# A graph layer with a running maximum over edges: later node search, casts on ScalarE, other end shares

## The chip, the cores and the metric

The kernel runs on one core of one Trainium2 chip. Its engines work side by side, each through its own list of instructions in order: TensorE (PE, and PEld for its weight loads), VectorE (DVE), ScalarE (ACT), GpSimd (POOL) and SyncE (SP), which only issues transfers. The metric is device time in microseconds of one execution.

## The reference

`N = 6250` nodes with rows of `D = 256` floats, `E = 100000` edges sorted by destination. For each edge a message is made, each node takes the largest of those that arrive, adds it to its row and normalises.

```python
x_src, x_dst = x[src], x[dst]
theta_x = (x_dst - x_src) @ theta_w.T + theta_b
phi_x = x_src @ phi_w.T + phi_b
e = relu(theta_x + phi_x)
out = segment_max(e, dst, num_segments=N)
out = where(isfinite(out), out, 0.0)
y = x + out
x = (y - mean(y)) / sqrt(var(y) + 1e-5)          # over the last axis
```

## The kernel before

The part of a message that hangs on the source is `B = x (phi - theta)^T`, one row per node. The part that hangs on the destination is the same for all edges of a node, so the kernel takes the maximum over `B[src]` first, and adds `x theta^T` and the biases, applies relu, adds `x` and normalises at the end. What has to be done fast is the maximum of 100000 rows by node. The kernel does it in three ways.

**First part.** The first 1130 nodes' edges are cut into 128 chunks of 146 steps, one chunk per partition. GpSimd gathers the rows of `B` by indirect transfers (L525, eight steps to a group), and VectorE runs a running maximum along each chunk (`run`, L687) that starts anew where the node changes. To read out a node's maximum one must know at which chunk and step its last edge stands: `node_place(j)` finds this for 128 nodes at a time, in nine blocks: two VectorE operations make a one-hot of the chunk (L843, L844), a matmul fetches that chunk's list of nodes (L846), and two `Sign` activations with an accumulated sum count how many entries lie before the node (L849); a copy takes the chunk's start (L852). `places_1` turns the counts into places. `chunk_heads` finds which chunks begin inside a node (L868 on), which `tails_1` (L889 on) needs to carry maxima across chunks.

**Second part, slots.** The other 5120 nodes are 128 partitions by 40 tiles. The rows of `B` are cut into 17 ranges of sources, the slots. `choice(s0)` picks, for two slots at a time (nine batches), at most one edge per node and slot: it marks the edges of a slot (L1016), takes minima (L1020 to L1025) to an int16 row number `at` (L1027), casts it to float in `chosen` (L1028), strikes that edge out (L1030, and L1034, which multiplies the marks of edges not yet used into `unused`). `wanted(s0)` transposes the codes by TensorE (L1041), copies them by ScalarE (L1043) and stores them. `slot_part`, in 85 chunks, loads the codes of one slot for eight tiles (L1080), lets ScalarE make one-hot matrices (an `Abs`, L1087, three times for 1024 columns each, then one `Relu`, L1090; later VectorE makes one of the three, L1085), multiplies them by the slot's rows of `B` on TensorE (24 matmuls, L1097) and takes the maximum into `acc` (ScalarE's copy L1106 for the first slot, then VectorE, L1108).

**Second part, list.** Edges that no slot took are counted and packed into a list of 233 steps (`list_pieces`, L1192 on: which are left, L1194; a cast to float, L1196; a scan that counts them, L1197; their ranks subtracted, L1206, and shifted by 20 bits, L1216; then a compaction by steps, L1225 and L1228). The list is gathered and reduced like the first part (30 groups, `run` with part 2, each group's maxima stored by SyncE at L699).

**Order.** Instructions of an engine run in the order in which the program issues them, apart from a few that `behind_in_order` puts behind a named one. The main program interleaves by hand: `next_group_1` issues a group of gathers of the first part, the running maxima of the group before, one `node_place` and some slot chunks. It is called from the loop over the list's pieces and after it. Then follow `places_1`, `tails_1` and the loop over the 30 list groups, in which the remaining slot chunks are spread evenly, with two shares of the first part's end from group 10 on. GpSimd's gathers wait for the rows that they overwrite.

**End.** `rows_of` and `normalise` handle a share of 8, 4 or 2 tiles: gathers of the maxima, matmuls with `theta` (L1335, L1338, L1347), VectorE adds (L1348, L1349, L1352, with the row's sum), the mean (L1365), ScalarE squares with their sum (L1368), then the variance (L1373), its inverse root with one Newton step (`inverse_root`, L423 to L429), the shift (L1375), and the result by ScalarE (L1383) or, for half the tiles of the last sixteen, VectorE (L1379), and the store (L1389). At the end the shares' widths are

```python
widths = [STEPS] * (TILES // STEPS - 2) + [4, 4, 4, 2, 2]
```

and two tiles are one piece of work; pieces and norms of different shares interleave.

## Time and profile before

| | us |
|---|---|
| three runs | 808.33, 814.1 (median), 823.09 |
| the profiled execution | 809.64 |
| its span, first to last instruction | 807.7 |

The mean granted TensorE clock of the profiled run is 0.913 of full speed. A row of a group of instructions has the line, the engine, the operation, output and inputs with their shapes, the count, then the busy time in us and the mean of one in ns, and behind the second bar the idle time of that engine just before these instructions with what ended most of it. A row of the timeline has start and length in us, and in brackets the idle time ahead with its releaser.

### The profile page before, as it was taken

What the parts mean: (1) busy time and instruction counts of PE and PEld (TensorE: products, weight loads), DVE (VectorE), ACT (ScalarE), POOL (GpSimd) and SP (SyncE); (2) the same over time, 40 slices, a digit from 0 to 9 for tenths busy, and PEclk for the clock granted to TensorE, in tenths of its full rate; (3) what the DMA queues carried; (4) which work ended last, traced back from release to release, by engine and by line L of the source; (5) the groups of instructions that cost most, each with busy time, mean ns of one, the idle gap of its engine ahead of it and who ended that gap; (6) DMA issues with size and microseconds to landing.
All of it is one profiled execution on the core that took longest, in us unless ns stands there. A gap on an engine that the chain in (4) does not pass through costs nothing.

```text
span 807.7 us, 9215 instructions
## 1 busy us (share of the span) xinstructions
PE 650.3 (81%) x2720; PEld 513.5 (64%) x2720; DVE 609.6 (75%) x1185; ACT 493.6 (61%) x576; POOL 475.1 (59%) x465
## 2 busy tenths in 40 slices
PE   5999787888874689399895988978999598677881
PEld 4888565656663478287774776756777376455771
DVE  7999989899956397278694686856698468783776
ACT  1446788997955375267574666745487377520666
POOL 7801888885676644436576766756656575425640
PEclk9999898999996989799997999989999899887896
DMA  8996638566685568346775777856858569644664
GB/s 275 310 367 223 187 107 265 161 186 221 217 266 187 160 225 288 104 131 210 232 243 166 229 266 264 291 169 214 250 175 268 169 204 318 210 151 124 206 239 159
DMA packets 60365, 174.40 MB, mean 216 GB/s; under 512 B 11995, under 2 KB 19956, under 8 KB 53268
## 3 DMA queue, kind: packets, MB, share of 16 engines
q1 hardware_dynamic: 37240, 109.25, 39.3%
q0 software_dynamic: 20944, 57.62, 24.2%
q10 hardware_dynamic: 2124, 6.88, 2.4%
q8 instruction: 23, 0.38, 0.2%
q14 instruction: 34, 0.28, 0.1%
HBM read 105.52 MB, written 68.18 MB: 215 GB/s over the span
## 4 chain that ended last, share of the span: by engine, by line
PE 42%; DVE 18%; issue 13%; another core or an unknown queue 11%; ACT 9%; DMA 4%; POOL 2%; DVEq 0%; SPq 0%; ACTq 0%; POOLq 0%
PE ps_f L1097 32%; PE ps_b L779 6%; DVE g L687 6%; ACT hot L1087 3%; DVE acc L1108 3%; ACT hot L1090 3%; DMA g<-maxima,place 2%; POOL g L525 2%; DVE hot L1085 1%; PE ps_e L1338 1%; ACT x_f L1383 1%; DVE x_f L1352 1%; DMA g<-b_rows,list_src 1%; DVE g L1348 1%
## 5 line engine op out<-in xcount | busy, mean ns | idle before, releaser
L1097 PE MATMUL ps_f<-hot,terms 128*128 128x512 f32 x1960 | 497.9, 412 | 92.7 <-ACT hot L1090 33.1
L1097 PEld LDWEIGHTS ps_f<-hot,terms 128*128 128x128 f32 x1960 | 383.7, 199 | 198.8 <-issue 47.1
L525 POOL DMA_INDIRECT g<-b_rows,list_src x232 | 234.0, 1009 | 154.1 <-DVE g L687 61.0
L1087 ACT ACTIVATE hot<-want,minus_row 128x1024 fp32r<-128x1024 f16 x187 | 205.3, 1145 | 186.7 <-remote 94.4
L1108 DVE TENSOR_TENSOR acc<-acc,ps_f 128x1024 f32<-128x1024 f32 x160 | 193.7, 1215 | 138.6 <-remote 75.9
L525 POOL DMA_INDIRECT g<-b_rows,src x130 | 153.8, 1183 | 97.0 <-DMA want<-chosen_rows 38.2
L687 DVE SCALAR_TENSOR_TENSOR g<-g,caps 128x256 f32<-128x256 f32 x376 | 180.3, 480 | 3.6
L1090 ACT ACTIVATE hot<-hot 128x2048 fp32r<-128x2048 f32 (+2 forms) x85 | 177.5, 2088 | 1.8
L779 PE MATMUL ps_b<-weights,x_t 128*128 128x256 f32 x260 | 62.8, 396 | 1.2 <-ACT x_t L767 0.6
L525 POOL DMA_INDIRECT g<-maxima,place x40 | 38.1, 953 | 42.9 <-DVE acc L1108 17.8
L779 PEld LDWEIGHTS ps_b<-weights,x_t 128*128 128x128 f32 x260 | 49.8, 197 | 10.4 <-ACT x_t L767 4.0
L1368 ACT ACTIVATE squares<-x_f,r 128x256 bf16<-128x256 f32 x49 | 24.2, 495 | 45.5 <-DVE r L1365 40.9
L1338 PE MATMUL ps_e<-weights,kept 128*128 128x256 f32 x160 | 42.9, 414 | 1.7 <-issue 1.7
L1085 DVE TENSOR_SCALAR hot<-want,row_id 128x1024 fp32r<-128x1024 f16 x58 | 44.1, 760 | 0.0
L1338 PEld LDWEIGHTS ps_e<-weights,kept 128*128 128x128 f32 x160 | 34.0, 212 | 7.2 <-issue 2.0
L1348 DVE TENSOR_TENSOR g<-g,ps_e 128x512 f32<-128x512 f32 x20 | 13.7, 685 | 25.9 <-remote 16.3
L782 ACT COPY b_sb<-ps_b 128x512 f32<-128x512 f32 (+1 forms) x25 | 14.5, 580 | 27.0 <-PE ps_b L779 19.0
L525 POOL DMA_INDIRECT g<-in_x_dram,src x16 | 25.3, 1582 | 5.6 <-issue 4.4
L1383 ACT ACTIVATE x_f<-x_f,r 128x256 f32<-128x256 f32 x41 | 21.5, 588 | 7.2 <-DVE r L1375 4.4
L767 ACT COPY x_t<-ps_xt 128x512 f32<-128x512 f32 (+1 forms) x33 | 18.4, 588 | 8.1 <-PE ps_xt L764 7.6
L1335 PE MATMUL ps_e<-bias_terms,pick 128*128 128x512 f32 x20 | 10.6, 528 | 9.9 <-DVE g L1348 8.6
L1228 DVE COPY_PREDICATED work<-words,work 128x288 int32<-128x288 int32 (+9 forms) x11 | 16.7, 1515 | 0.0
(253 smaller groups left out, 421.9 us busy)
## 6 DMA issues: line engine op xcount, KB each, us to landing
maxima<-g SPq DMA_DIRECT2D x47, 1024.0 KB
want<-chosen_rows SPq DMA_DIRECT2D x85, 256.0 KB
x_q<-in_x_dram SPq DMA_DIRECT2D x12, 512.0 KB
b_rows<-b_sb ACTq DMA_DIRECT2D x12, 512.0 KB
x_columns<-x_t SPq DMA_DIRECT2D x20, 256.0 KB
kept<-x_columns SPq DMA_DIRECT2D x10, 512.0 KB
raw<-b_rows SPq DMA_DIRECT2D x16, 256.0 KB
x_f<-in_x_dram SPq DMA_DIRECT2D x4, 1024.0 KB
```

Of the source, the lines that this page charges most:

```text
L525: one = nc.gpsimd.indirect_dma_start(out=to, out_offset=None, in_=table, in_offset=bass.IndirectOffsetOnAxis(ap=offsets, axis=0))
L687: one = nc.vector.scalar_tensor_tensor(g[:, k, :], last[part], caps[:, t : t + 1], g[:, k, :], op0=ALU.min, op1=ALU.max)
L779: nc.tensor.matmul(ps[:, h, :], x_t[:, h, k, :], weights[:, k, 0, :], start=(k == 0), stop=(k == KC - 1))
L1085: nc.vector.tensor_scalar(hot[:, b, :], want, row_id[:, b : b + 1], None, op0=ALU.is_equal)
L1087: nc.scalar.activation(hot[:, b, :], want, AF.Abs, bias=minus_row[:, b : b + 1], scale=1.0)
L1090: nc.scalar.activation(apart, apart.bitcast(FP), AF.Relu, bias=1.0, scale=-1.0)
L1097: nc.tensor.matmul(ps[:, w : w + 512], terms[:, part, b, h * P : (h + 1) * P], hot[:, b, w : w + 512], start=(i == 0), stop=(i == n - 1),)
L1108: one = nc.vector.tensor_tensor(to, to, ps, op=ALU.max)
L1338: nc.tensor.matmul(a[:, i, :], x_t[:, 2 * i + c, :], weights[:, c, 1, :], start=False, stop=(i == w - 1 and c == KC - 1))
L1348: nc.vector.tensor_tensor(some, some, ps[:, :w, :], op=ALU.max)
L1368: nc.scalar.activation(squares, x_f[:, k, :], AF.Square, bias=mean[:, k : k + 1], scale=1.0, accum_out=var[:, k : k + 1])
L1383: nc.scalar.activation(x_f[:, k, :], x_f[:, k, :], AF.Identity, bias=mean[:, k : k + 1], scale=inv[:, k : k + 1])
```

## The change

The parts of the diff, in the order of a run:

- `choice`: the cast of `at` to `chosen` goes from VectorE to ScalarE, and `at` gets three buffers. For the first slot pair `unused` is made by one product of the two slots' marks, where before it was filled with ones and multiplied twice.
- `list_pieces`: the cast of the left-over marks goes to ScalarE; ScalarE multiplies the ranks by 2^20 in advance, behind its last copy of B; VectorE then subtracts the count times 2^20 in one operation, and the shift goes.
- `ends_1` (formerly straight code), `node_place` and `places_1` move from the first part's groups into the loop over the list groups: `ends_1` to group 0, one `node_place` to each of groups 0 to 8, `places_1` to group 9. `chunk_heads` moves to directly ahead of `tails_1`.
- `run`: the list's last full group is stored in three pieces, after four, six and eight steps.
- `normalise`: the division by D goes into the squares' scale (1/16 ahead of squaring), eps into the root's bias, so the steps for the variance and for adding eps go.
- The end's widths become 4, 4, 8, 8, 8, 4, 2, 2 instead of 8, 8, 8, 4, 4, 4, 2, 2.

```diff
+ROOT_D = 16.0
@@ -605,7 +606,9 @@
     iota(minus_row, -P, 0, -1)
     iota(columns[:, 0, :], Q1, 0, 0)
     iota(columns[:, 1, :], 1, P * Q1, 0)
-    bad = const.tile([P, 10], FP, name="bad")
+    checks = const.tile([P, 11], FP, name="bad")
+    bad, eps = checks[:, :10], checks[:, 10:]
+    nc.vector.memset(eps, EPS)
     descents = search.tile([P, T + 1], FP, name="descents")
     below = search.tile([P, T + 1], FP, name="below")
@@ -677,7 +680,7 @@
     def run(part, g, n, caps, t0, to, gathers=(), carry_row=None):
-
+        stored, ends_at = 0, (4, 6) if t0 + n == LIST_CHUNK else ()
         for k in range(n):
             t = t0 + k if part == 1 else LIST_CHUNK - 1 - t0 - k
             if last[part] is not None:
@@ -695,8 +698,13 @@
                     behind_in_order(one, latest_part[0], "VectorE's order")
                 used.append(one.ins.name)
             last[part] = g[:, k, :]
+            if part == 2 and k + 1 in ends_at:
+                a, ends_at = ends_at[0], ends_at[1:]
+                nc.sync.dma_start(to[:, stored:a, :], g[:, stored:a, :])
+                stored = a
         latest_run[0] = one.ins.name
-        nc.sync.dma_start(to, g[:, :n, :])
+        if stored < n:
+            nc.sync.dma_start(to[:, stored:n, :], g[:, stored:n, :])
     def run_1(i, gathers=()):
         t0, n = groups[i]
@@ -779,7 +789,7 @@
                     nc.tensor.matmul(
                         ps[:, h, :], x_t[:, h, k, :], weights[:, k, 0, :], start=(k == 0), stop=(k == KC - 1)
                     )
-            nc.scalar.copy(to, ps[:, :n, :])
+            b_copied[0] = nc.scalar.copy(to, ps[:, :n, :]).ins.name
         def x_group(i):
             for q in range(0, STEPS, 2):
@@ -817,19 +827,22 @@
     iota(offset[:, :Q1], 1, 0, 0)
     nc.vector.memset(offset[:, Q1:], 0.0)
     first = const.tile([P, 1], FP, name="first")
-    nc.vector.tensor_copy(first, chunk[:, 0:1])
-    nc.vector.memset(first[0:1, :], -1.0)
-
     low = const.tile([P, NT1], FP, name="low")
-    nc.vector.tensor_scalar(low, offset, -1.0, first, op0=ALU.mult, op1=ALU.add)
     high = const.tile([P, NT1], FP, name="high")
-    nc.vector.tensor_scalar(high, offset, -1.0, after, op0=ALU.mult, op1=ALU.add)
-    nc.vector.tensor_scalar(
-        bad[:, 2:3], after, float(N1), ident[:, P - 1 :], op0=ALU.is_lt, op1=ALU.mult
-    )
     upper = const.tile([P, 2, NT1], FP, name="upper")
-    nc.vector.tensor_scalar(upper[:, 0, :], node_1, 0.5, None, op0=ALU.add)
-    nc.vector.tensor_scalar(upper[:, 1, :], node_1, -0.5, None, op0=ALU.add)
+
+    def ends_1():
+
+        nc.vector.tensor_copy(first, chunk[:, 0:1])
+        nc.vector.memset(first[0:1, :], -1.0)
+        nc.vector.tensor_scalar(low, offset, -1.0, first, op0=ALU.mult, op1=ALU.add)
+        nc.vector.tensor_scalar(high, offset, -1.0, after, op0=ALU.mult, op1=ALU.add)
+        nc.vector.tensor_scalar(
+            bad[:, 2:3], after, float(N1), ident[:, P - 1 :], op0=ALU.is_lt, op1=ALU.mult
+        )
+        nc.vector.tensor_scalar(upper[:, 0, :], node_1, 0.5, None, op0=ALU.add)
+        nc.vector.tensor_scalar(upper[:, 1, :], node_1, -0.5, None, op0=ALU.add)
+
     signs = const.tile([P, 2, NT1], FP, name="signs")
     origin = const.tile([P, NT1], FP, name="origin")
     place_1 = const.tile([P, NT1], I32, name="place_1")
@@ -938,8 +951,7 @@
         return part if len(shape) == 2 else part.rearrange("p (s n) -> p s n", s=shape[1])
     chosen = index.tile([P, NS, TILES], FP, name="chosen")
-    at = index.tile([P, BATCH_S, 1, TILES], I16, name="at")
-    nc.vector.memset(unused, 1)
+    nc.vector.memset(unused[:, CHOICE_R * TILES :], 1)
     def floor_of(to, value, divisor):
         nc.vector.tensor_scalar(
@@ -1017,6 +1029,7 @@
         lowest = wide_i16(BATCH_S * CHOICE_R * W, [P, BATCH_S, CHOICE_R * W // 2])
         low = lowest[:, :n, :]
+        at = index.tile([P, BATCH_S, 1, TILES], I16, name="at", bufs=3)
         least = lambda to, a, b: nc.vector.tensor_tensor(to, a, b, op=ALU.min)
         least(low, in_slot[:, :n, : 12 * W], in_slot[:, :n, 12 * W :])
         least(low[:, :, : 6 * W], low[:, :, : 6 * W], low[:, :, 6 * W :])
@@ -1025,13 +1038,15 @@
         least(low[:, :, :W], low[:, :, :W], low[:, :, 2 * W : 3 * W])
         nc.vector.tensor_scalar(at[:, :n, 0, :], low[:, :, :W], rows_in(s0), None, op0=ALU.min)
-        nc.vector.tensor_copy(chosen[:, s0 : s0 + n, :], at[:, :n, 0, :])
+        nc.scalar.copy(chosen[:, s0 : s0 + n, :], at[:, :n, 0, :])
         kept = in_slot.rearrange("p s (r j) -> p s r j", r=CHOICE_R)
         nc.vector.tensor_tensor(
             kept[:, :n], kept[:, :n], at[:, :n].to_broadcast([P, n, CHOICE_R, W]), op=ALU.not_equal
         )
         for i in range(n):
-            one = nc.vector.tensor_tensor(unused[:, all_ranks], unused[:, all_ranks], in_slot[:, i, :], op=ALU.mult)
+            rest = in_slot[:, 1, :] if s0 + i == 0 else unused[:, all_ranks]
+            if s0 + i != 1:
+                one = nc.vector.tensor_tensor(unused[:, all_ranks], rest, in_slot[:, i, :], op=ALU.mult)
         ahead_of_run[0] = one.ins.name
     def wanted(s0):
@@ -1193,7 +1208,9 @@
         left_over = wide_i16(3 * BATCH_S * CHOICE_R * TILES // 2, [P, TR])
         nc.vector.scalar_tensor_tensor(left_over, padded, float(SLOT * NS), unused, op0=ALU.is_lt, op1=ALU.mult)
         valid, count = work_1, work_2
-        nc.vector.tensor_copy(valid.rearrange(by_node, r=R), left_over.rearrange("p (r j) -> p j r", r=R))
+        nc.scalar.copy(valid.rearrange(by_node, r=R), left_over.rearrange("p (r j) -> p j r", r=R))
+        one = nc.scalar.activation(order, order, AF.Copy, scale=float(1 << 20))
+        behind_in_order(one, b_copied[0], "B ahead of the ranks")
         nc.vector.tensor_tensor_scan(count, valid, valid, 0.0, ALU.add, ALU.max)
         nc.vector.tensor_copy(n_list, count[:, TR - 1 :])
         sums = sums_of_lists()
@@ -1203,7 +1220,7 @@
         list_chunks(sums)
         nc.vector.tensor_scalar(bad[:, 3:4], n_list, float(OWN_LIST), None, op0=ALU.is_gt)
         distance, mask = order.bitcast(I32), count.bitcast(I32)
-        nc.vector.tensor_tensor(distance, order, count, op=ALU.subtract)
+        nc.vector.scalar_tensor_tensor(distance, count, -float(1 << 20), order, op0=ALU.mult, op1=ALU.add)
         nc.vector.tensor_scalar(mask, valid, -1.0, None, op0=ALU.mult)
         word = words.bitcast(I32)
         nc.vector.tensor_tensor(
@@ -1213,7 +1230,6 @@
             op=ALU.add,
         )
         done = valid.bitcast(I32)
-        nc.vector.tensor_scalar(distance, distance, 20, None, op0=ALU.logical_shift_left)
         nc.vector.tensor_tensor(done, word, distance, op=ALU.bitwise_or)
         nc.vector.tensor_tensor(done, done, mask, op=ALU.bitwise_and)
         yield
@@ -1362,17 +1380,21 @@
         shared = part == 2 and j0 >= TILES - 2 * STEPS
         r = work.tile([P, 5, STEPS], FP, name="r", bufs=4)
         mean, var, root, inv, step = (r[:, k, :n] for k in range(5))
-        nc.vector.tensor_scalar(mean, totals[:, :n], -1.0 / D, None, op0=ALU.mult)
+        nc.vector.tensor_scalar(mean, totals[:, :n], -1.0 / (D * ROOT_D), None, op0=ALU.mult)
         for k in range(n):
             squares = work.tile([P, D], BF, name="squares")
             nc.scalar.activation(
-                squares, x_f[:, k, :], AF.Square, bias=mean[:, k : k + 1], scale=1.0, accum_out=var[:, k : k + 1]
+                squares, x_f[:, k, :], AF.Square, bias=mean[:, k : k + 1], scale=1.0 / ROOT_D, accum_out=var[:, k : k + 1]
             )
             if k % 2 and k + 1 < n:
                 yield
-        nc.vector.tensor_scalar(var, var, 1.0 / D, None, op0=ALU.mult)
-        inverse_root(nc, inv, var, root, step)
-        nc.vector.tensor_tensor(mean, mean, inv, op=ALU.mult)
+        nc.scalar.activation(root, var, AF.Sqrt, bias=eps)
+        nc.vector.reciprocal(inv, root)
+        nc.vector.tensor_tensor(step, inv, inv, op=ALU.mult)
+        nc.vector.scalar_tensor_tensor(step, var, EPS, step, op0=ALU.add, op1=ALU.mult)
+        nc.vector.tensor_scalar(step, step, -0.5, 1.5, op0=ALU.mult, op1=ALU.add)
+        nc.vector.tensor_tensor(inv, inv, step, op=ALU.mult)
+        nc.vector.scalar_tensor_tensor(mean, mean, ROOT_D, inv, op0=ALU.mult, op1=ALU.mult)
         yield
         for k in range(n):
             if shared and k % 2:
@@ -1433,8 +1455,6 @@
             gathers = gather_group(i, b_rows)
             if i > X_GROUPS:
                 run_1(i - 1, gathers)
-        if todo:
-            node_place(todo.pop(0))
         fetch_parts(n)
     fill_table()
@@ -1448,7 +1468,6 @@
         run_1(i)
     for _ in range(2):
         next_group_1(0)
-    chunk_heads()
     for i, _ in enumerate(list_pieces()):
         if i == 14:
             dve_hots[0] = DVE_HOTS
@@ -1466,10 +1485,10 @@
     tables.close()
     x_ring = body.enter_context(tc.tile_pool(name="x_ring", bufs=X_RING, side="right"))
     kept_ring = body.enter_context(tc.tile_pool(name="kept_ring", bufs=3, side="right"))
-    while groups_1 or todo:
+    while groups_1:
         next_group_1(2)
     run_1(len(groups) - 1)
-    places_1()
+    chunk_heads()
     carried = tails_1()
     n_groups = LIST_GROUPS
     blocks_left = lambda: sum(blocks_in(s) for s, _ in parts)
@@ -1491,6 +1510,11 @@
             next(heads, None)
         if i == CARRY_AT:
             carry_row = gather_carry()
+            places_1()
+        if i == 0:
+            ends_1()
+        if todo:
+            node_place(todo.pop(0))
         g, gathers = gather_2(i * STEPS)
         if i:
             run(2, g_before, STEPS, caps_2, (i - 1) * STEPS, maxima_2t[i - 1], gathers)
@@ -1515,7 +1539,7 @@
     fetch.close()
     ps_end = body.enter_context(tc.tile_pool(name="ps_end", bufs=6, space=PSUM))
-    widths = [STEPS] * (TILES // STEPS - 2) + [4, 4, 4, 2, 2]
+    widths = [4, 4] + [STEPS] * (TILES // STEPS - 2) + [4, 2, 2]
     assert sum(widths) == TILES
     last_shares = [(2, sum(widths[:i]), n) for i, n in enumerate(widths)]
     at_end = Shares(lambda: ps_end.tile([P, 2 * D], FP, name="ps_e"))
```

More of the change, by code (lines that the diff above doesn't have):

```diff
@@ L768, in x_transposed @@
             return x_t
+        b_copied = [None]
         def b_of(to, rows, kept=None):
@@ L1295, in gather_carry @@
         return carry_row
+    assert ROOT_D * ROOT_D == D
     x_tiles = {}
```

## The prediction

> **What bounds the kernel now.** I read the page first (busy times, chain), then the waits, then a table of busy time by stage, then the groups and the timeline of the stages that the diff touches.
>
> ```profile
> span 807.7 us, 9215 instructions
> PE 650.3 (81%) x2720; PEld 513.5 (64%) x2720; DVE 609.6 (75%) x1185; ACT 493.6 (61%) x576; POOL 475.1 (59%) x465
> ...
> PE 42%; DVE 18%; issue 13%; another core or an unknown queue 11%; ACT 9%; DMA 4%; POOL 2%; DVEq 0%; SPq 0%; ACTq 0%; POOLq 0%
> ```
>
> No engine is full over the whole span. TensorE carries 42% of the chain that ended last, VectorE 18%, ScalarE 9%. These are means over unlike stages, so I cut the span at the first slot sums (98), the end of the list's making (240), the start of the list gathers (340) and the last slot maximum (722). Columns are start and end, length, busy time of the five engines with counts, granted clock, DMA share and GB/s.
>
> ```profile
> core 0: us, PE busy (x) PEld busy (x) DVE busy (x) ACT busy (x) POOL busy (x), PEclk, DMA share, GB/s
> 0.00:98.00 98.00, 83.11 (x408) 68.91 (x408) 90.43 (x183) 47.17 (x81) 48.70 (x56) 0.97 0.81 276
> 98.00:240.00 142.00, 120.55 (x483) 93.65 (x483) 127.95 (x254) 123.03 (x132) 104.79 (x85) 0.93 0.65 204
> 240.00:340.00 100.00, 64.53 (x254) 51.11 (x254) 60.31 (x105) 50.76 (x39) 56.34 (x60) 0.84 0.60 195
> 340.00:722.00 382.00, 325.85 (x1315) 253.83 (x1315) 278.36 (x445) 235.20 (x206) 229.07 (x227) 0.93 0.67 219
> 722.00:808.00 86.00, 56.25 (x260) 46.02 (x260) 52.57 (x201) 37.47 (x120) 36.21 (x38) 0.81 0.53 177
> ```
>
> VectorE sets the first stage (90.4 of 98). In the second VectorE (128), ScalarE (123) and TensorE (121 of 142) are all near full, and each is waited for by turns. In the list stage TensorE is busy 326 of 382 and the other two have room: 104 us on VectorE, 147 on ScalarE. The waits show by turns who is late:
>
> ```profile
> POOL g L525 <- DVE g L687: 82.4, 25, 18.7
> ACT hot L1087 <- remote: 94.4, 16, 14.3
> DVE acc L1108 <- remote: 75.9, 14, 10.7
> PE ps_f L1097 <- ACT hot L1090: 33.1, 16, 14.5
> PE ps L1041 <- DVE chosen L1028: 4.8, 1, 4.8
> ```
>
> Columns: total, times, longest. The two "remote" rows (170 us together) are ScalarE and VectorE waiting for something that the profile cannot name; each follows slot matmuls, so I read them as late releases by TensorE. No edit touches those matmuls: I leave this time where it is. The last row is one wait of the first stage that the change aims at.
>
> **The change, part by part.** The sum is made against the profiled run, 809.64 us (span 807.7). The three plain runs are 808.33, 814.1 and 823.09, so that run lies 4.5 below their median.
>
> *First stage: codes converted by ScalarE, one product less.*
>
> ```profile
> L1028 DVE CAST chosen<-at 128x80 f32<-128x80 int16 x8 | 1.6, 201 | 0.3
> L1034 DVE TENSOR_TENSOR unused<-unused,wide 128x960 int16<-128x960 int16 x17 | 11.2, 659 | 0.4
> L844 DVE SCALAR_TENSOR_TENSOR hot<-columns,high,hot 128x128 f32<-128x128 f32 x9 | 3.0, 337 | 0.0
> L843 DVE TENSOR_SCALAR hot<-columns,low 128x128 f32<-128x128 f32 x9 | 2.7, 299 | 0.9 <-PE ps L846 0.9
> ```
>
> ```profile
> 98.42 0.79 PE L1097 MATMUL ps_f<-hot,terms 128*128 128x512 f32 x1 [0.68 <-ACT g L782]
> ```
>
> This is the first slot sum, the end of the stage. By the pace of the batches six of the nine casts (L1028) lie before 98: 6 x 0.201 = 1.2 us off VectorE. The first two products (L1034) become one: 0.66 us. Of the node search, nine pairs of L843 and L844 (2.7 + 3.0 = 5.7 us), some two pairs run here (an estimate from the code's order): 1.3 us. Together 3.2 us off the engine that is 92% full. On ScalarE (47 of 98) the casts are a small matter, but they add a wait: a code now goes VectorE, ScalarE, TensorE, and the cast stands in ScalarE's order among the copies of B, so each copy behind it waits until VectorE has that batch. ScalarE has 51 us of idle time here, which covers this; uncovered, it would cost up to the one wait of 4.8 above, on the other side. I take -3, bounds 0 (transfers or GpSimd set this stage: the DMA share is 0.81) to -3.2, and +4.8 as the bad end.
>
> *Second stage: node search out, list's casts to ScalarE, shift gone.* The next rows are the groups of this stage, then its timeline on VectorE and GpSimd (start, length, operation, idle time before).
>
> ```profile
> L849 ACT ACTIVATE junk<-ps,upper 128x146 bf16<-128x146 f32 x18 | 6.7, 378 | 1.4 <-PE ps L846 1.0 <-issue 0.4
> L849 ACT ACTIVATION_READ_ACCUMULATOR junk<-ps,upper 128x1 f32 x18 | 3.6, 200 | 0.0
> L1106 ACT COPY acc<-ps_f 128x1024 f32<-128x1024 f32 x10 | 10.1, 1011 | 5.3 <-issue 3.6 <-PE ps_f L1097 1.6
> L846 PE MATMUL ps<-ids,hot 128*128 128x148 f32 x18 | 4.4, 326 | 1.2 <-DVE hot L844 1.2
> ...
> L1216 DVE TENSOR_SCALAR order<-order 128x1440 int32<-128x1440 int32 x1 | 0.9, 910 | 0.0
> ```
>
> ```profile
> 113.77 1.64 DVE L1194 SCALAR_TENSOR_TENSOR wide<-padded,unused 128x1440 int16<-128x1440 int16 x1
> ...
> 115.74 1.61 DVE L1196 CAST work<-wide 128x1440 f32<-128x1440 int16 x1
> ...
> 117.67 3.14 DVE L1197 TENSOR_TENSOR_SCAN work<-work 128x1440 f32<-128x1440 f32 x1
> ```
>
> ```profile
> 112.76 0.94 POOL L525 DMA_INDIRECT g<-b_rows,src  x1 [0.30 <-issue]
> 114.01 3.46 POOL L525 DMA_INDIRECT g<-b_rows,src  x1 [0.30 <-issue]
> 117.78 3.79 POOL L525 DMA_INDIRECT g<-b_rows,src  x1 [0.30 <-issue]
> ...
> 206.72 0.94 POOL L525 DMA_INDIRECT g<-b_rows,src  x1 [12.03 <-DVE g L687]
> ```
>
> VectorE loses the other seven pairs (5.7 x 7/9 = 4.4), the cast L1196 (1.6), the shift L1216 (0.9) and three small casts (0.6): 7.5 us. ScalarE loses the eighteen Signs, between 6.7 (accumulator reads beneath) and 10.3 us; I take 8, nearer the first because the recorded ends overlap. It gains the cast and the scaling of 1440 columns. No such row exists; by the 1024-column copy (1.011 us) each is 1.011 x 1440/1024 = 1.4 us, two 2.8. The three small casts lie between the accumulator read (0.20) and the 146-column Sign (0.38): 0.9 in all. So ScalarE goes from 123.0 to 123.0 - 8 + 2.8 + 0.9 = 118.7, 4.3 less. TensorE's 120.6 loses the eighteen search matmuls, 4.4 us. The stage can shrink by what the less relieved of the two loses, 4.3; I take -4, bounds 0 and -7.5. The new wait: the scan L1197 now waits for ScalarE's cast, which stands in its order behind one chunk's Relu; what is queued behind the scan on VectorE is the list's counting and the first part's running maxima, and GpSimd's gathers wait for those. At worst that is one such wait of a few us, inside the 0 end of this term. What becomes late next is TensorE: it has 21 us of idle time in this stage, so the gain has room.
>
> *Third stage.* It is a chain (last rows of the first part, tails, caps) with no engine above 65 of 100 us. The moved chunk heads add some 1 us of small VectorE work ahead of the tails, under 60 us of work in 100. It passes earlier gains on: 0.
>
> *List stage: the search comes in here.* Each of groups 0 to 8 gets two VectorE operations (0.64 us), a matmul pair on TensorE and two Signs on ScalarE (0.9 us). That is 8 us on ScalarE, which has 147 us idle, 6 us on VectorE, which has 104, and the 4.4 us on TensorE, which is the bound. I take +2, since TensorE's 56 us of idle time hide part. Queues passed: the search issues no DMA; SP's queue gets two more DMAs for the split store; GpSimd's first gather by these places comes after group 9, with a group's length (382/30 = 12.7 us) between. Lower bound 0, upper bound in the second rival.
>
> *Three-piece store.*
>
> ```profile
> 719.77 0.94 POOL L525 DMA_INDIRECT g<-maxima,place  x1 [17.79 <-DVE acc L1108]
> ```
>
> The first gather behind the list's store waits for VectorE's last slot maximum, not for the store, so an earlier store buys nothing while the slots end at 722: 0, bounds 0 and -1.5.
>
> *End: norm and shares.*
>
> ```profile
> 747.39 0.51 ACT L1368 ACTIVATE squares<-x_f,r 128x256 bf16<-128x256 f32 x1 [34.45 <-DVE r L1365]
> ...
> 788.94 5.03 ACT L1383 ACTIVATE x_f<-x_f,r 128x256 f32<-128x256 f32 x10 [1.38 <-DVE r L1375]
> ```
>
> ```profile
> L423 DVE TENSOR_SCALAR r<-r 128x8 f32<-128x8 f32 (+2 forms) x8 | 1.5, 189 | 0.0
> ...
> L1373 DVE TENSOR_SCALAR r<-r 128x8 f32<-128x8 f32 (+2 forms) x8 | 1.3, 161 | 0.0
> ```
>
> Two of nine VectorE steps of a norm go (L423, L1373): 2.8 us over eight norms, of which the last norm's 0.35 us is surely on the path, the rest only as far as VectorE is pressed (53 of 86). The widths matter more. ScalarE stands idle for 34 us until the first norm of eight tiles, then has a backlog: at 788.94 it applies ten tiles in 5 us, late in the stage. A first share of four tiles brings the first norm forward by two of twenty pieces; at (789 - 722)/20 = 3.4 us a piece that is 7 us of earlier work for ScalarE, and about half of the backlog (2.5 us) should be gone. 0.35 + 2.5 is 2.9: I take -3, bounds +2 (eight-wide shares now stand later, so the 4, 2, 2 at the end meet more unfinished work) and -6.
>
> Sum: -3 - 4 + 0 + 2 + 0 - 3 = -8, 809.6 - 8 = 801.6; I say 802.
>
> **The rivals.** *GpSimd sets the first 240 us.*
>
> ```profile
> L525 POOL DMA_INDIRECT g<-b_rows,src x130 | 153.8, 1183 | 97.0 <-DMA want<-chosen_rows 38.2
> ```
>
> The first part's 130 gathers take 1.18 us each, and two of them 3.46 and 3.79 where the neighbour takes 0.94. If their issue is the pace, less work on VectorE and ScalarE is only more waiting: the first two terms fall away, 809.6 + 2 - 3 = 808.6. Against it: at 206.72 GpSimd itself waits 12 us for a running maximum on VectorE. In this case the long gathers count: the one at 114.01 ends at 117.47, 0.12 us after the cast L1196 (117.35), the next at 121.57, 0.76 us after the scan (120.81). With the cast on ScalarE the first would end with L1194 at 115.41, 2 us sooner: 806.6. The Trainium skill ("SBUF — State Buffer", section "SBUF: two separate sides") calls this a lock: while VectorE holds the port pair that it shares with GpSimd, GpSimd writes no descriptors for its DMAs. The trace agrees for the cast by these 0.12 us; the scan's gather runs on for longer than the rule says. I give this rival 0.17.
>
> *The search stops ScalarE in the list stage (slower).* In the list stage a Sign stands in ScalarE's order between the slots' one-hots, and its matmul stands in TensorE's order behind a chunk's matmuls. If ScalarE has run ahead it must wait there for TensorE, and the next chunk's one-hots come late. A wait of TensorE on one-hots costs 33.1/16 = 2.1 us on the mean; nine of them 19 us in place of the +2, so 809.6 - 10 + 19 = 818.6. It decides against the change from 10/9 = 1.1 us a node on. For it: TensorE already waits sixteen times for L1090. Against: ScalarE is 62% busy here, and two buffers of one-hots keep it from running far ahead, so it mostly waits for the same releases already. 0.15.
>
> *More than the sum.* If the 12 us wait at 206.72 goes because VectorE's backlog of running maxima goes, stage two shrinks by the full 7.5, and if the end gives its 6: 809.6 - 3 - 7.5 + 2 - 6 = 795. 0.15.
>
> *The change doesn't do what it says*, since a scheduler places the moved work where it likes: the order of the built kernel has the nine searches among chunks 29 to 44, inside the list stage, so I give it nothing.
>
> **How the numbers follow.** The forecast has the remaining 0.53. The likeliest case gives 802. The range 788 to 820 holds it with its bounds, the GpSimd rival, the larger gain and most of the slower rival; below lies an end that gives more than 6 with a first stage that gives more than its casts, above a search of over 2.2 us a node. Two per cent of 814.1, about what these runs can tell from no change, puts the borders at 798 and 830. Faster: 0.12 of the larger gain and 0.15 out of the forecast's lower part, 0.27. Slower: 0.03 of the slower rival's tail and 0.06 for runs that spread as 823 did, 0.09. Same: 0.64.
>
> **What would show it.** First stage: the wait of L1041 shrinks from 4.8 and the slot sums begin some 3 us sooner than 98. Second: no Sign rows before 240, VectorE near 120 busy, the 12 us wait at 206.72 below 8, the list gathers 7 us sooner than now. List stage: from first list gather to last slot maximum 382 to 385 us; Signs with idle time in front of over 1 us each would prove the slower rival. End: 83 us, the first squares within 30 us of the last slot maximum, the ten-tile application gone. The prediction is wrong if the list stage grows by more than 6 us, or if the list gathers begin when they do now.

## The result, and the profile after

The changed kernel takes 819.92 us in the median of 20 executions (812.04 to 827.84), the kernel before 813.68 (799.94 to 828.91). The ratio is 1.0152 of the time before, 95% interval 1.0112 to 1.0193. Forecast were 802 us and a gain. The ratios, here and below, leave out executions over 1.5% above the fastest of their kernel (here 14 of the 20 of the kernel before and 2 of the changed one), while the medians are of all executions, by which the ratio would be 1.0077. The profiled execution of the changed kernel, 826.43 us (span 824.6), lies 6.5 above its median and that of the kernel before 4.0 below, so the two profiles differ by more than the kernels do.

The page, and the waits, of the changed kernel (total, times, longest):

```profile
span 824.6 us, 9185 instructions
PE 652.7 (79%) x2720; PEld 516.1 (63%) x2720; DVE 602.5 (73%) x1154; ACT 501.6 (61%) x587; POOL 489.9 (59%) x465
...
L526 POOL DMA_INDIRECT g<-b_rows,src x130 | 168.2, 1294 | 90.6 <-DMA want<-chosen_rows 41.0
```

```profile
ACT hot L1102 <- remote: 124.7, 17, 15.9
DVE acc L1123 <- remote: 123.9, 24, 15.8
```

VectorE has 7 us less to do, ScalarE 8 more. What was not foreseen is GpSimd: the same 130 gathers take 168.2 us where they took 153.8. The table by stretch shows where; the first fence is the kernel before, the second the changed one. The columns are those of the stage table above, and each stretch holds the list's compaction (eleven steps of a `TENSOR_SCALAR` and a `COPY_PREDICATED` on VectorE, L1225 and L1228 before, L1241 and L1244 after).

```profile
142.00:207.00 65.00, 55.67 (x223) 42.83 (x222) 60.94 (x87) 59.83 (x65) 42.92 (x35) 0.95 0.58 178
```

```profile
142.00:194.00 52.00, 48.07 (x202) 37.42 (x201) 52.00 (x70) 50.28 (x37) 45.65 (x21) 0.99 0.55 175
```

VectorE gets through the compaction in 52 us instead of 65, with no gap (52.00 of 52). In that time GpSimd issues 21 gathers of 2.2 us, where before it issued 35 of 1.2 us. The timeline of the changed kernel shows one such meeting after the other:

```profile
163.07 0.87 DVE L1241 TENSOR_SCALAR words<-work 128x1408 int32<-128x1408 int32 x1
165.79 1.75 DVE L1244 COPY_PREDICATED work<-words,work 128x1408 int32<-128x1408 int32 x1
171.76 0.86 DVE L1241 TENSOR_SCALAR words<-work 128x1376 int32<-128x1376 int32 x1
```

```profile
162.74 2.04 POOL L526 DMA_INDIRECT g<-b_rows,src  x1 [0.30 <-issue]
165.08 0.95 POOL L526 DMA_INDIRECT g<-b_rows,src  x1 [0.30 <-issue]
166.33 2.01 POOL L526 DMA_INDIRECT g<-b_rows,src  x1 [0.30 <-issue]
...
171.44 2.01 POOL L526 DMA_INDIRECT g<-b_rows,src  x1 [0.30 <-issue]
```

The three long gathers end at 164.78, 168.34 and 173.45, which is 0.84, 0.80 and 0.83 us after the ends of the three VectorE operations (163.94, 167.54, 172.62); the one that meets neither takes 0.95. No idle time of GpSimd over 1 us is left between 96 and 237: it sets the pace of the first part now. So the list is made 13 us earlier, and the first part, for whose rows its gathers wait, is later:

```profile
318.52 1.42 POOL L526 DMA_INDIRECT g<-b_rows,list_src  x1 [15.80 <-DVE g L690]
...
737.20 0.95 POOL L526 DMA_INDIRECT g<-maxima,place  x1 [18.93 <-DVE acc L1123]
```

The first list gather starts at 318.5 (before at 310.4), the first gather of the end at 737.2 (before at 719.8, the row in the prediction). Of the 16.9 us between the two spans 8.1 are there at the list's first gather, 9.3 come in the list stage, and the end gives 0.5 back. How much of this is the change and how much the draw, only more profiles can tell.

### The profile page after: what moved, and what is told of

It reads as the page before. It is cut to its first block, busy times and chain, and to the rows that moved or that the text cites. A ratio compares the mean times of both kernels' runs of the same rounds, so it can differ in the third digit from the quotient of the medians.

```text
span 824.6 us, 9185 instructions
## 1 busy us (share of the span) xinstructions
PE 652.7 (79%) x2720; PEld 516.1 (63%) x2720; DVE 602.5 (73%) x1154; ACT 501.6 (61%) x587; POOL 489.9 (59%) x465
## 4 chain that ended last, share of the span: by engine, by line
PE 38%; DVE 18%; issue 13%; another core or an unknown queue 12%; ACT 7%; DMA 6%; POOL 6%; DVEq 0%; POOLq 0%; ACTq 0%; SPq 0%
PE ps_f L1112 32%; POOL g L526 6%; DVE g L690 4%; DMA g<-b_rows,src 3%; PE ps_e L1356 2%; DVE acc L1123 2%; DVE words L999 2%; ACT hot L1102 2%; ACT hot L1105 1%; ACT squares L1386 1%; DMA g<-b_rows,list_src 1%; ACT x_f L1405 1%; DVE work L996 1%; DVE wide L1033 1%
## 5 line engine op out<-in xcount | busy, mean ns | idle before, releaser
L1112 PE MATMUL ps_f<-hot,terms 128*128 128x512 f32 x1960 | 506.9, 417 | 112.7 <-DVE acc L1123 32.1
L1112 PEld LDWEIGHTS ps_f<-hot,terms 128*128 128x128 f32 x1960 | 389.2, 202 | 221.6 <-issue 59.7
L1123 DVE TENSOR_TENSOR acc<-acc,ps_f 128x1024 f32<-128x1024 f32 x160 | 193.8, 1216 | 169.6 <-remote 123.9
L526 POOL DMA_INDIRECT g<-b_rows,src x130 | 168.2, 1294 | 90.6 <-DMA want<-chosen_rows 41.0
L690 DVE SCALAR_TENSOR_TENSOR g<-g,caps 128x256 f32<-128x256 f32 x376 | 180.7, 481 | 3.7
L1356 PE MATMUL ps_e<-weights,kept 128*128 128x256 f32 x160 | 41.1, 400 | 1.7 <-issue 1.7
L1366 DVE TENSOR_TENSOR g<-g,ps_e 128x512 f32<-128x512 f32 x20 | 13.7, 684 | 21.7 <-remote 12.6
L526 POOL DMA_INDIRECT g<-in_x_dram,src x16 | 22.7, 1421 | 5.7 <-issue 4.1
L1244 DVE COPY_PREDICATED work<-words,work 128x288 int32<-128x288 int32 (+9 forms) x11 | 16.8, 1530 | 0.0
```

Source lines behind the costliest of these rows:

```text
L526: one = nc.gpsimd.indirect_dma_start(out=to, out_offset=None, in_=table, in_offset=bass.IndirectOffsetOnAxis(ap=offsets, axis=0))
L690: one = nc.vector.scalar_tensor_tensor(g[:, k, :], last[part], caps[:, t : t + 1], g[:, k, :], op0=ALU.min, op1=ALU.max)
L1112: nc.tensor.matmul(ps[:, w : w + 512], terms[:, part, b, h * P : (h + 1) * P], hot[:, b, w : w + 512], start=(i == 0), stop=(i == n - 1),)
L1123: one = nc.vector.tensor_tensor(to, to, ps, op=ALU.max)
L1356: nc.tensor.matmul(a[:, i, :], x_t[:, 2 * i + c, :], weights[:, c, 1, :], start=False, stop=(i == w - 1 and c == KC - 1))
```

## The experiments

They ran in five groups, each on one chip with the kernel before beside it. The chips differ by more than the kernels do, so ratios and medians are compared within a group.

**First group: which part.** The conversions back on VectorE, the search back in the first part, and two parts alone on the kernel before:

```diff
 e1, on the changed kernel: node search, ends, places, chunk heads where they were
 e2, on the changed kernel:
-        nc.scalar.copy(chosen[:, s0 : s0 + n, :], at[:, :n, 0, :])
+        nc.vector.tensor_copy(chosen[:, s0 : s0 + n, :], at[:, :n, 0, :])
-        nc.scalar.copy(valid.rearrange(...), left_over.rearrange(...))
-        one = nc.scalar.activation(order, order, AF.Copy, scale=float(1 << 20))
-        behind_in_order(one, b_copied[0], "B ahead of the ranks")
+        nc.vector.tensor_copy(valid.rearrange(...), left_over.rearrange(...))
 (and the subtraction and the shift as before)
 e3, on the kernel before: the moved search alone
 e4, on the kernel before: seven-step norm, widths, three-piece store
```

> The changed kernel with the node search (its ends, the nine blocks, the places and the chunk heads) back among the first part's gathers. Theory G (GpSimd): with the search and the casts gone from VectorE, the list's large operations stand closer together and each gather that meets them takes longer (2.03 us each from 140 to 200 where before had 1.20), so the first part ends 7 us late. Then the search's small operations part them again: gathers of 1.2 to 1.5 us there, the last gather of the first part near 295 instead of 302, and a ratio to the kernel before of 0.995 to 1.005. Theory A (ScalarE): the scan's 5.8 us wait for the cast of 3.1 us, and the waits of 6.3 and 3.6 us of the slot sums behind it, are the loss; the search's place matters nothing: gathers still near 2 us, ratio 1.010 to 1.020. Theory L (list stage): the search's nine blocks cost 10 us between chunks 30 and 60 of the slots; that stretch falls from 222 to about 210 us, and the last gather of the first part stays near 302.

> The changed kernel with the three conversions (codes, left-over marks, ranks with the shift) back on VectorE. Theory G: VectorE gets 4 us back, but the search is still away, so the gathers from 140 to 200 stay at 1.7 us or more and the ratio to before at 1.006 to 1.015. Theory A: the scan starts at 117 to 118 instead of 122, the 6 us waits go, and the ratio falls to 0.995 to 1.003. Theory L: no change, 1.010 to 1.018.

> The kernel before with nothing but the moved search. Theory G: gathers from 140 to 200 slower than 1.2 us, 1.5 to 2.0, and a ratio of 1.008 to 1.015. Theory A: 0.995 to 1.002. Theory L: the first part ends no later than 295, the stretch from chunk 30 to chunk 60 is 10 us longer, ratio 1.010 to 1.015.

> The kernel before with the seven-step norm, the end's new widths and the store in three pieces, and nothing else. All three theories: up to 722 as before, then an end 2 to 3 us shorter than the 85 us from the first end piece on (the changed kernel has 82): ratio 0.996 to 0.998. If the end's gain is only a shift of a few rows in a late profile, 1.000.

| run | median us | ratio to before (828.79) | interval |
|---|---|---|---|
| e1, search back | 845.99 | 1.0195 | 1.0131 to 1.0258 |
| e2, conversions back | 822.70 | 0.9927 | 0.9865 to 0.9988 |
| e3, search alone | 835.84 | 0.9972 | 0.9902 to 1.0042 |
| e4, end alone | 832.30 | 1.0063 | 1.0001 to 1.0126 |

The search alone changes nothing that shows (e3). Put back in the changed kernel, it does not bring the time down, but e1 has a trouble of its own, in its waits:

```profile
ACT g L792 <- remote: 23.5, 4, 8.0
```

Four copies of B wait 23.5 us there for releases that no instruction in the profile accounts for. Its first slot sum starts at 126.4 instead of 98, so e1 says little about the search. With the conversions back on VectorE (e2) the kernel is 0.7% faster than before, which makes them the suspects. It is no more than that yet: the changed kernel did not run in this group, and the kernel before against itself (h1 below) came out 0.8% apart. The end's 2 to 3 us of gain did not show. Theory G in its first form falls: search and conversions were to act alike on the gathers, and they did not (1.35 us each during the compaction in e3, 1.31 in e2, by the timelines, and 1.75 in e1, where the search is back).

**Second group: which conversion.** On e2, one conversion at a time goes back to ScalarE, and the changed kernel stands beside them.

> The version with the three conversions on VectorE (0.993 of before), with the codes' casts alone given back to ScalarE. Theory K (codes): each cast stands in ScalarE's order between copies of B and one-hots and waits there for VectorE, so ScalarE and TensorE behind it fall back; this one carries most of the 2.2% between the version with the conversions on VectorE and the changed kernel: ratio 1.005 to 1.015. Theory M (marks): none of it, 0.990 to 0.997. Theory G (gathers): the ratio follows the gathers from 140 to 200; over 1.7 us each there with a ratio over 1.005, or near 1.25 us with a ratio under 0.998.

> The same version with the cast of the left-over marks alone given to ScalarE. Theory M: the cast takes 3.1 us on ScalarE instead of 1.6 on VectorE and comes behind a chunk's one-hots, VectorE waits some 6 us for it at the scan, and what follows the list is late: ratio 1.000 to 1.008. Theory K: 0.990 to 0.996. Theory G: as for the codes, the gathers from 140 to 200 decide.

> The same version with the ranks alone scaled by ScalarE and the shift gone. Theories K and M: 1.4 us on ScalarE against 0.9 us off VectorE, no wait: 0.991 to 0.996, as without it. If it is this one that holds the slot sums back (it stands ahead of the first slots' copies), 1.003 or more.

> The changed kernel once more, on the same chip as the three parts of the conversions: ratio 1.010 to 1.020. Theory G: gathers from 140 to 200 again near 2 us, and no wait of GpSimd over 1 us between 100 and 240. If the first profile was a chance one, gathers near 1.25 us and the same ratio, which would clear GpSimd.

| run | median us | ratio to before (833.75) | interval | compaction, us | mean gather in it, us | first list gather |
|---|---|---|---|---|---|---|
| f1, codes | 806.98 | 0.9690 | 0.9627 to 0.9753 | 60.4 | 1.28 | 299.2 |
| f2, marks | 813.94 | 0.9788 | 0.9734 to 0.9841 | 63.0 | 1.30 | 302.4 |
| f3, ranks | 817.76 | 0.9789 | 0.9717 to 0.9861 | 62.9 | 1.33 | 305.4 |
| f4, all three | 825.12 | 0.9883 | 0.9813 to 0.9953 | 51.6 | 2.14 | 320.4 |

(The last three columns are read from the timelines: from the first `COPY_PREDICATED` to the last one's end, and the gathers that overlap it.) The codes, on which theory K laid the loss, cost nothing: f1 is the fastest here. Marks and ranks on top of the codes cost 18.1 us in the medians, and the lowest execution of f4 (815.51) is above the highest of f1 (814.62). At the first list gather they cost 21.2 us. The first part's gathers, in f1 and then in f4:

```profile
L526 POOL DMA_INDIRECT g<-b_rows,src x130 | 155.1, 1193 | 93.1 <-DMA want<-chosen_rows 42.8
```

```profile
L526 POOL DMA_INDIRECT g<-b_rows,src x130 | 168.1, 1293 | 95.3 <-DMA want<-chosen_rows 44.0
```

In this group the long wait for the marks is there only when all three are together: the scan's idle time in front, in f2 and in f4,

```profile
L1210 DVE TENSOR_TENSOR_SCAN work<-work 128x1440 f32<-128x1440 f32 x1 | 3.2, 3158 | 0.5 <-ACT work L1209 0.5
```

```profile
L1214 DVE TENSOR_TENSOR_SCAN work<-work 128x1440 f32<-128x1440 f32 x1 | 3.2, 3160 | 5.1 <-ACT work L1211 5.1
```

The changed kernel is faster than before in this group, although its profile has the same slow gathers as the first: what the kernel before takes depends on the chip (814, 829, 834), the changed kernel much less (820, 825).

**Third group: pairs, on a chip that is different in kind.** The changed kernel without the ranks, without the marks, without the codes, and with none of the three.

> The changed kernel without the scaled ranks (the subtraction and the shift as before); codes and marks on ScalarE. Theory W (the wait at the scan): the changed kernel loses because ScalarE comes late with the marks and VectorE waits 5 us for it; codes, ranks and marks together make ScalarE late. Without the ranks' 1.4 us the wait at the scan is 1 to 5 us, the slot sums' first chunks wait less, and the ratio lies between that of the three on VectorE and that of the changed kernel, 0.5% or more over the former. Theory X (the list's work and the gathers meet): the wait itself costs little; what costs is that the gathers from 140 to 200 take 1.9 us in place of 1.2, and the loss comes only with those: gathers over 1.7 us and 1.5% over the three on VectorE, or near 1.2 us and no loss.

> The changed kernel with the marks' cast alone back on VectorE. Theory W: no wait at the scan, and the loss is gone: within 0.5% of the three on VectorE, or below. Theory X: as for the last, the gathers from 140 to 200 and the ratio go together. If the ranks in front of the first slots' copies are the loss, 1% or more over the three on VectorE with gathers near 1.2 us.

> The changed kernel with the codes alone back on VectorE. Theory W: VectorE loses 1.7 us and ScalarE gains 2.4, so the wait at the scan falls from 5 to about 1 us or none, and the ratio comes within 0.7% of the three on VectorE. Theory X: gathers from 140 to 200 and ratio together again.

> The three conversions on VectorE once more, as the foot of the comparison on this chip: between 0.970 and 0.995 of before, by the two chips seen so far; scan at 115 to 116 without a wait, gathers from 140 to 200 near 1.2 us.

| run | median us | ratio to before (694.55) | interval | compaction, us | mean gather in it, us | first list gather |
|---|---|---|---|---|---|---|
| g1, codes and marks | 691.46 | 0.9975 | 0.9949 to 1.0002 | 59.5 | 1.33 | 285.5 |
| g2, codes and ranks | 699.22 | 1.0066 | 1.0039 to 1.0094 | 57.6 | 2.46 | 296.8 |
| g3, marks and ranks | 699.11 | 1.0070 | 1.0042 to 1.0099 | 58.0 | 1.58 | 285.5 |
| g4, none | 696.88 | 1.0046 | 1.0018 to 1.0075 | 63.1 | 1.32 | 284.8 |

Here every kernel takes some 120 to 140 us less, and the profiles list no wait on "remote". The meeting of compaction and gathers is the same as elsewhere, as g2's stretch shows:

```profile
135.00:193.00 58.00, 51.81 (x217) 39.91 (x217) 55.51 (x75) 57.12 (x41) 51.60 (x22) 1.00 0.54 175
```

with 22 gathers in 51.6 us, and its list starts 11 us later than g1's. But g2's profiled execution (707.96 us) is one of two near 708, and the other eleven lie between 695 and 702. That the gathers slip past the compaction in those eleven would explain it, but no profile of one was kept, so it is a guess. In g2's profile the gathers are slow without the marks' cast and without a wait at the scan, so they do not need theory W's wait. The times decide nothing between the theories: g2, g3 and g4 lie within 0.3% of each other, as W forecast for g2, and g3 has gathers of 1.58 us and an early list where theory X wants both or neither.

**Fourth group: before, after, search and codes on one chip.**

> The kernel before once more, with a profile on this chip: ratio 1.000. It shows which kind of chip this is: waits on releases of TensorE that the profile calls remote over 100 us (a span of 800 to 840), or none (a span near 693). Theory X (list work and gathers meet): gathers from 140 to 200 near 1.2 us.

> The changed kernel once more. Theory X: gathers from 140 to 200 near 1.9 us, the first list gather 8 us or more later than in the version with the codes alone, and the end as much later. From the pairs on the last chip the three conversions add up to no more than -0.1% of their absence there (codes -0.4, marks -0.3, ranks +0.6), so without the slow gathers the ratio would be 1.003; with them 1.010 to 1.020.

> The kernel before with the moved search alone, once more: 0.995 to 1.002, gathers from 140 to 200 near 1.25 us. A ratio over 1.005 would put a part of the loss on the search in the list stage.

> The changed kernel with marks and ranks back on VectorE (codes on ScalarE, the search moved, the end changed). Theory X: gathers from 140 to 200 near 1.2 us, the first list gather 8 us or more earlier than in the changed kernel, and the ratio 1% to 2% below that of the changed kernel on this chip; against before 0.97 to 0.98 on a chip with late releases, 0.998 to 1.003 on one without.

| run | median us | ratio to before (836.24) | interval | compaction, us | mean gather in it, us | first list gather |
|---|---|---|---|---|---|---|
| h1, before again | 838.30 | 1.0081 | 1.0006 to 1.0156 | 66.3 | 1.28 | 327.0 |
| h2, changed | 826.83 | 0.9799 | 0.9710 to 0.9889 | 51.6 | 2.13 | 318.1 |
| h3, search alone | 834.46 | 1.0003 | 0.9892 to 1.0113 | 66.0 | 1.30 | 318.7 |
| h4, codes | 809.94 | 0.9819 | 0.9691 to 0.9947 | 61.8 | 1.28 | 300.2 |

h1 against itself gives 1.008, so nothing under 1% counts here. By the ratios h2 and h4 are alike. Three executions of h2 lie between 806 and 818 and make its ratio; the other nine, the profiled one among them, lie between 824 and 831, and so its median is 2% above that of h4. The two profiles differ by 17.9 us at the first list gather and by 17.8 in the span (825.5 and 807.7): all of it is made before the list stage. The profile of h1 shows what the first one of the kernel before did not:

```profile
126.11 0.29 DVE L843 TENSOR_SCALAR hot<-columns,low 128x128 f32<-128x128 f32 x1 [13.72 <-remote]
```

VectorE stands 13.7 us at a search operation, and the choice's last product (L1034) and the list's work are queued behind it; the list starts at 327.0 instead of 310.4. In the first profile the same line had waited 0.9 in all. The moved search takes this place away, yet h3 shows no gain, so it is not settled that this is why the kernel before is slow on some chips.

**Fifth group: filler on VectorE.** It came on the chip of the third group again.

```diff
+        def fill():
+            for _ in range(2):
+                spare = work.tile([P, P], FP, name="hot_1").bitcast(I32)
+                nc.vector.tensor_tensor(spare, done[:, :P], done[:, P : 2 * P], op=ALU.bitwise_or)
...
+            fill()
             one = nc.vector.copy_predicated(done[:, :n], moves[:, :n], done[:, shift : shift + n])
+            fill()
```

> The changed kernel with 44 small VectorE operations (128 columns, about 0.28 us each, 12 us in all) put between the steps of the list's compaction; they write a tile that nobody reads. Theory X: the compaction lasts 58 to 64 us again instead of 52, the gathers that run during it take 1.6 us or less instead of 2.2, the first list gather comes 5 to 15 us earlier than in the changed kernel, and the time falls by 0.5% to 1.5% against it, although VectorE has 12 us more to do. Theory Y (the slow gathers only go with something else, such as ScalarE's casts, and VectorE's time counts): the time rises by 0.5% to 1.5%, or stays.

> The changed kernel once more, beside the one with filler: gathers during the compaction near 2.2 us. Ratio to before 0.98 to 0.99 on a chip with late releases where before stands near 835, 1.010 to 1.020 where before stands near 814, 1.003 to 1.015 on a chip without late releases (before near 694).

k1 gives 699.19 us, 1.0088 of before (1.0053 to 1.0123), k2 699.98 us, 1.0040 (1.0003 to 1.0077), with 693.53 before. The stretches of the compaction, k1 and then k2:

```profile
136.00:209.00 73.00, 66.14 (x278) 50.87 (x276) 73.00 (x129) 70.68 (x50) 59.79 (x38) 1.00 0.62 197
```

```profile
135.00:187.00 52.00, 48.10 (x201) 37.39 (x200) 52.00 (x72) 50.35 (x37) 46.56 (x18) 0.98 0.50 167
```

The gathers go from 2.6 to 1.6 us, and the first list gather from 297.8 to 290.8, both as theory X has it. The compaction became longer than meant, 73 us, and the time did not fall. It stayed, as the rival theory Y has it: the 11.4 us more of VectorE work (44 operations of 280 ns) cost nothing in the median and 0.5% by the ratios, whose intervals overlap. k2's executions lie from 690.65 to 703.41, and the profiled one, with the slow gathers, took 702.86. Its scan waits only 0.4 us for the marks, so here too the gathers are slow without theory W's wait.

## Why the prediction was wrong

**First stage (-3).** The first slot sum starts at 97.8 instead of 98.4, and between 94.6 and 98.3 in the other runs with codes on ScalarE, but for e1. With the codes on VectorE it starts between 96.0 and 101.2, and the means of the two sets are 1.9 us apart. The sign was right, the size smaller, and the casts' wait of 4.1 us on VectorE (ScalarE, three times) did no harm.

**Second stage (-4): the step that failed.** It said that the stage shrinks by what the less relieved of VectorE and ScalarE loses, with TensorE as the next limit. VectorE did get faster, but GpSimd became the limit: the compaction without gaps made its gathers longer by some 14 us (168.2 against 153.8), and the list's first gather came 8.1 us later, not 7 earlier. The prediction had the mechanism in hand, in its GpSimd rival, but read from two gathers only what a cast's removal gives back. It did not ask what VectorE's operations do to GpSimd when they come closer together. The Trainium skill ("SBUF — State Buffer", section "SBUF: two separate sides") says that GpSimd and a VectorE operation in a two-port mode exclude each other, and it counts `tensor_scalar` among the operations that can run so. It puts the end of a blocked transfer about 0.1 us after the operation's. The trace agrees that the gathers wait, but `COPY_PREDICATED` held them too, and they ended 0.80 to 0.84 us after either operation.

What the runs show of this: in all four profiles of the changed kernel (the first, f4, h2, k2) the gathers take 2.1 to 2.7 us and the compaction 52 us. In every profile with a compaction of 59 us or more they take at most 1.35 us, but for the filler's 1.6; in the three between (e1, g2, g3) 1.6 to 2.5. The four profiles of the changed kernel are of executions above its median in their group, by 0.5 to 6.5 us, so they may show the meeting oftener than it happens. With marks and ranks taken out, the list starts 18 to 21 us earlier in two groups. That the two, on top of the codes, cost time is shown in the second group (f1 against f4), on one chip; in the fourth the medians differ the same way by 2%, but the ratios do not.

That the slow gathers are the path to this loss is argued, not shown: in f4 they take 13 us more than in f1, and the list starts 21 us later, but the filler, on the chip without "remote" waits, undid most of the slow gathers without a gain. Nor do the 8.1 us of the first pair measure it. With the first part as it was, the list starts at 310.4, at 321.4 (e4) and at 327.0 (h1); the changed kernel's, in the first profile, f4 and h2, starts at 318 to 320. So the prediction's -4 is not what was found, and how much later than before the changed kernel's list starts on a given chip stays open.

**Marks' cast.** A size was off too: 1.4 us by the copy from PSUM.

```profile
118.90 3.11 ACT L1211 CAST work<-wide 128x1440 f32<-128x1440 int16 x1
...
122.05 3.16 DVE L1214 TENSOR_TENSOR_SCAN work<-work 128x1440 f32<-128x1440 f32 x1 [5.77 <-issue]
```

It takes 3.1 us, twice VectorE's 1.6 (the scaling of the ranks, on as many columns, took 1.41, as put), and the scan that waits for it stands 5.8 us, where the working had put "a few us, inside the 0 end of this term".

**List stage (+2).** The rival that ends slower had the search stop ScalarE here. The Signs hardly wait (window of the list stage):

```profile
L862 ACT ACTIVATE junk<-ps,upper 128x146 bf16<-128x146 f32 x18 | 6.6, 371 | 0.3 <-PE ps_f L1112 0.3
```

0.3 us for all eighteen, where that rival had put 19 us. The 9.3 us by which this stage is longer in the first pair of profiles, more than the 6 that the prediction named as a sign of being wrong, come from the profile of the kernel before. From the first list gather to the first of the end it is 418.7 us in the changed kernel, 417.6 in f4 and 418.4 in h2, but 422.7 in h1 and 425.8 in e4, where the search is in the first part as before. Why the first profile of the kernel before has 409.4 was not found.

**Store (0) and end (-3).** From the first gather of the end it is 87.4 instead of 87.9 us, and e4 gave 1.0063. From the last slot maximum the old end takes 85.0 to 86.0 us (before, e3, h1, h3), the new one 82.0 to 85.4 on chips of that kind: at most a part of the 3.

**Late releases.** The prediction read the 170 us of "remote" waits as late releases by TensorE, which no row shows, and left them where they were, as something that no edit touches. They are no constant: 249 us in the profile after, none on the chip of the third group. What else the measured loss holds is mixed up with them and stays open, as does the chip's part in the sign of the result (0.98 to 0.99 on two chips, 1.004 on one, 1.015 in the result). That 819.92 us still lies inside the stated 788 to 820 is luck: none of the prediction's cases describes what the profiles show.

**A version that may beat both.** The changed kernel with the marks and ranks back on VectorE (f1, h4): 0.969 and 0.982 of before. Against the changed kernel it is 2% faster in the second group; in the fourth it is so by the medians and not by the ratios. On the chip of the third group it wasn't run; there codes and marks together (g1) are the fastest at 0.9975, within its interval of before.

## What to carry to other kernels

Before an engine is relieved, list which other engines it holds up, and ask what happens when its operations close up: VectorE's int32 operations made GpSimd's gathers wait, and in the stretch without gaps GpSimd issued 21 gathers where it had issued 35. Price a stage by the engine that would be last after the edit, with its instruction times taken from where the two meet, not from where they are alone. And where a kernel's time moves by 15% between chips, compare kernels on one chip, and read a profile as one draw among several.

## What the runs showed of the hardware

Not every VectorE operation holds up a gather. The one at 165.08 in the changed kernel's first profile took 0.95 us, although a maximum from PSUM (L1123, 1.20 us at 164.27) and a running maximum (L690, 0.47 us at 165.40) ran across it; the three that met an int32 `TENSOR_SCALAR` or `COPY_PREDICATED` took 2.0.

Long waits on "remote", for which the profile names no releaser, stand in the profiles of some chips and not of others. The same changed kernel spans 824.6 us with the two "remote" rows of 249 us, and 701.0 us on the chip of the third and fifth groups, where the waits have no such row; the kernel before takes 814 to 836 us and 694. The mean granted clock goes along (0.903 and 0.96), but that alone is 6% of TensorE's time: TensorE is busy for 652.7 and 614.3 us, 38 us apart, where the spans are 124 apart.
